# A fused Fourier-mixer block on one core: the order of all operations from a list scheduler that models the five queues

## The chip, the core and the metric

The kernel runs on one core of a Trainium2 chip. The core has five engines with a queue each: TensorE (PE, with its weight loads as PEld), VectorE (DVE), ScalarE (ACT), GpSimd (POOL) and SyncE (SP, which here only issues transfers). Each works through its own queue in the order in which the program was built, and semaphores make it wait for the others. The metric is the device time of one execution in microseconds (us), lower is better. Before the change the median of 3 runs is 2781.52 us (2774.99 to 2794.49).

## What is computed

The input is `x`, 8 x 128 x 128 x 96 in float32. After a layer norm over the channels, a filter in frequency space and a residual, a second layer norm feeds a small two-layer network on values rounded to 8-bit floats, and a second residual ends the block. Cut to what matters:

```
x_pre = soa(einsum('bhwc,mc->bhwm', x, w1))            # 96 -> 192 channels; soa(x) = scale * relu(x)^2 + bias
xf    = rfft2(x_pre)                                   # over h and w, 128 x 65 frequencies
filt  = [Rh @ cw_s @ Rw for s in range(3)]             # three small complex filters, resized to 128 x 65
gctx  = x.mean((h, w)); sctx = relu(bn(x @ sp_w.T)).mean((h, w))
r     = softmax(mlp([gctx, sctx]), over the 3 filters) # per batch and channel
comb  = einsum('shwm,bsm->bhwm', filt, r)
out   = einsum('bhwm,cm->bhwc', irfft2(xf * comb), w2)
```

and for the network `y = qlinear(relu(qlinear(z, W1, b1)), W2, b2)` with 96 -> 384 -> 96 channels, where both operands of a product are rounded to fp8 (5 exponent bits) and sums to fp16.

## The kernel before

The Fourier transforms are matrix products with constant matrices. The work of each of the 8 batches is cut into three streams that pass their results through DRAM.

- **Stream a** (`before`, from L618), 32 steps u of 4 columns. Layer norm statistics are made on DVE (`measure`, L635) and POOL; the factor goes to DRAM and comes back spread over partitions (`store_r`, `load_r`, L643 to L649), `scale` (DVE, L651) applies it to the transposed input `zT`. `project` (PE, L663, writes `px`), `rectify` and `square` (ACT) and `context` (POOL) make `x_pre`; `transform` (PE, `py`, L693) is the transform over h; `put` (ACT) and `store_y` write Y to DRAM. At the end of a batch nine small steps `rate_*` (L744 to L805) make the softmax weights.
- **Stream s** (`spectrum`, from L825), 33 groups g of frequencies. `load_y` (SP, four transfers a group) and `load_t` fetch Y and the filters `tb`; `weigh` (POOL, L855) applies the batch's weights; `along_w` (PE, `pz`, L863) is the transform over w; `filters_of` (PE, `pf`, L865) resizes the filters; `copy_sr` (ACT), `make` and `times` (DVE, L900 and L903), `turn_back` and `real_basis` (POOL) multiply by the filter. For each of 16 pairs p of groups, `mix_low` and `mix` (PE, `pv`, L958) project 192 channels to 96, `mixed` (ACT) copies, `invert` (PE, `pg`, L978) transforms back, `inverted` (ACT) copies, `store_v` writes V.
- **Stream c** (`after`, from L1066), 32 steps u in 8 blocks of 4. `load_v` fetches x and V, `last` (PE, `pk`) is the last transform back, `residual` and `measure` (DVE) follow, then the layer norm's `variance`, `root`, `inverse`, `rest`; `quantise` (ACT, for the last batch half of it on DVE), `turn` (PE, transposes), `turned` (DVE), `first` (PE, `ph`), `accumulated` (ACT), `biased` (DVE), `hidden` (ACT), `second` (PE, `po`), `put` (ACT), `bias` (DVE), `add_up` (POOL), `store`.

Stream s of a batch needs all of its stream a, and stream c all of its stream s. So in the middle of the run stream a of one batch, stream s of the one before and stream c of the one before that are interleaved. `filters_of`, `mix_low` and `mix` use 64 columns of PE's array with 52 or 64 rows, so that four products share it (the 64-wide tiling); all other products use the whole array or take it as one tile.

**What sets the order.** Each operation is handed to `at` (L388) with a wished time, the operations that it needs (`after`), how many of the 6 PSUM banks it takes and which operations set them free (`until`). Wished times are written out: a start and a length for each stream of each batch (`STREAMS`), and an offset in steps for each kind of operation (`O`, with own tables for four of the streams, `OWN`). `in_order` (L323) takes from a heap the operation with the lowest time whose needs have been taken, and skips one for which no bank is free:

```
place[follower.key] = max(place[follower.key], place[op.key] + lag)   # lag 0.15, or 2.28 for a transfer
heappush(ready, (place[follower.key], follower.seq, follower))
```

It has no notion of how long an operation lasts or of what its engine is doing. The list that comes out is built in that order, and L1243 ties each engine's instructions to it. Waits on data, and on buffers that are used again, are added as the program is built.

## Time and profile before

| | us |
|---|---|
| median of 3 runs | 2781.52 (2774.99 to 2794.49) |
| the profiled execution | 2788.19 |
| its span | 2786.4 |
| mean granted PE clock in it | 0.958 of full |
| DMA queue of SP, of ACT: share of 16 engines' span | 60.7%, 14.4% |
| PE waiting on its longest named cause (`px` for the scaled `zT`) | 38.5 |
| SP waiting for stores of `t` (POOL), for Y's buffers (PE `pz`), for the norm's factor to come back | 266.0, 200.3, 106.5 |

The profile lists matmuls under the tile that they write: `px`, `py`, `pz`, `pf`, `pv`, `pg`, `pk`, `ph`, `po` as named above (`pz<-ident` is the transpose `turn`). A float32 product has two records. An engine's busy time is the union of its records; PE's records overlap, [...]so the length of one is more than what it takes from PE. "Idle before" is an engine's idle time ahead of an operation, and the name after the arrow is what ended it.

### The profile page before, as it was taken

To read this page: it belongs to the slowest core of one execution; us is meant where nothing else is said; L and a number is where in the kernel's file an instruction comes from. 1 tells how busy PE (TensorE), PEld (TensorE's weight loads), DVE (VectorE), ACT (ScalarE), POOL (GpSimd) and SP (SyncE) were. 2 spreads that over 40 slices of the span, in tenths; PEclk is the share of its full clock that TensorE was granted. 3 is DMA by queue.
4 is the path that set the end of the run, shared out by engine and by line. 5 is a ranking of instruction groups with operands and counts; after the bars stand their busy time and mean duration, and the time that the engine had idled before them with its cause. 6 is when DMAs were issued, how large, how long until landed. Compare 5 with 4: busy or idle time off the path is not lost.

```text
span 2786.4 us, 80592 instructions
## 1 busy us (share of the span) xinstructions
PE 2545.2 (91%) x30762; PEld 1887.8 (68%) x30762; DVE 2035.8 (73%) x5110; ACT 2210.3 (79%) x4452; POOL 2063.5 (74%) x2983
## 2 busy tenths in 40 slices
PE   4879999999999999999999999999999998898665
PEld 2557777677677767776677777777767776676433
DVE  3346666577877778786787779677887768888686
ACT  2665555588888888888998878789988987788887
POOL 2228886778788877887788869888788886998432
PEclk9899999999999999999999999999999998999886
DMA  7888888978689867887788858888788775665431
GB/s 203 258 253 241 245 247 240 268 224 250 204 256 260 232 202 219 255 252 225 234 253 267 238 167 236 261 257 254 236 244 264 216 212 168 182 192 159 159 125 46
DMA packets 752818, 620.43 MB, mean 223 GB/s; under 512 B 578367, under 2 KB 654023, under 8 KB 752411
## 3 DMA queue, kind: packets, MB, share of 16 engines
q1 hardware_dynamic: 697138, 464.28, 60.7%
q10 hardware_dynamic: 55296, 151.02, 14.4%
q8 instruction: 244, 4.00, 0.6%
q14 instruction: 140, 1.14, 0.1%
HBM read 406.99 MB, written 208.16 MB: 221 GB/s over the span
## 4 chain that ended last, share of the span: by engine, by line
PE 60%; ACT 10%; POOL 9%; DMA 9%; DVE 6%; issue 5%; SPq 1%; ACTq 0%; POOLq 0%; DVEq 0%
PE px L666 12%; PE pz L863 9%; PE py L695 9%; PE pv L958 8%; PE pf L874 5%; PE pg L980 4%; PE ph L1128 3%; PE pk L1085 3%; PE po L1150 3%; ACT y L1135 3%; POOL t L1168 2%; ACT h L1143 2%; DMA tb<-T 2%; ACT z L1109 2%; POOL rr L911 2%
## 5 line engine op out<-in xcount | busy, mean ns | idle before, releaser
L911 POOL TENSOR_TENSOR rr<-t,t 128x390 f32<-128x390 f32 x512 | 536.7, 1058 | 58.5 <-DVE t L904 57.5
L666 PE MATMUL px<-W1S,zT 97*128 97x240 f32 x2048 | 521.7, 380 | 44.1 <-DVE zT L653 38.5
L1109 ACT ACTIVATE z<-t,ln_m,ln_r 128x96 fp8e5<-128x96 f32 x960 | 465.1, 495 | 43.5 <-DMA zT<-in_xT 11.7
L1135 ACT CAST y<-ph 128x512 f16<-128x512 f32 x768 | 458.0, 606 | 37.4 <-PE ph L1128 19.4
L666 PEld LDWEIGHTS px<-W1S,zT 97*128 97x128 f32 x2048 | 377.0, 194 | 141.9 <-issue 37.7
L863 PEld LDWEIGHTS pz<-F,yt 128*128 128x128 f32 x3120 | 417.0, 194 | 82.3 <-DVE t L1091 9.0
L863 PE MATMUL pz<-F,yt 128*128 128x130 f32 x3120 | 443.0, 282 | 13.2 <-DVE t L1091 6.0
L695 PE MATMUL py<-X,F 128*128 128x384 f32 x1024 | 432.1, 509 | 8.6 <-ACT yst L702 3.9
L677 ACT ACTIVATE rl<-px 128x480 f32<-128x480 f32 x512 | 296.3, 582 | 179.1 <-PE px L666 147.8
L1143 ACT ACTIVATE h<-y 128x1536 fp8e5<-128x1536 f16 x256 | 387.5, 1514 | 5.5 <-DVE y L1139 3.8
L857 POOL TENSOR_TENSOR tb<-tb,r 128x384 f32<-128x384 f32 (+1 forms) x264 | 296.7, 1124 | 124.3 <-DMA tb<-T 66.7
L1168 POOL TENSOR_TENSOR t<-t,o 128x1536 f32<-128x1536 f32 x64 | 206.1, 3221 | 188.9 <-DVE o L1165 185.3
L904 DVE TENSOR_TENSOR t<-dm,pf 128x390 f32<-128x390 f32 x512 | 283.2, 553 | 68.8 <-PE pf L874 39.0
L1139 DVE TENSOR_TENSOR y<-y,b1q 128x1536 f16<-128x1536 f16 x256 | 288.2, 1126 | 56.1 <-ACT y L1135 55.5
L958 PEld LDWEIGHTS pv<-w2C,xf 64*64 64x64 f32 x12288 | 274.2, 136 | 77.0 <-issue 32.9
L958 PE MATMUL pv<-w2C,xf 64*64 64x96 f32 x12288 | 315.8, 251 | 7.3 <-ACT yst L702 2.8
L1128 PE MATMUL ph<-zT,W1q 96*128 96x512 fp8e5 x768 | 297.4, 401 | 22.2 <-DVE zT L1124 8.8
L702 ACT COPY yst<-py 128x384 f32<-128x384 f32 x512 | 248.0, 490 | 70.1 <-PE py L695 57.6
L904 DVE TENSOR_TENSOR t<-dp,pf 128x390 f32<-128x390 f32 x512 | 280.6, 548 | 0.0
L928 POOL TENSOR_TENSOR xf<-rr 128x378 f32<-128x378 f32 x256 | 263.0, 1027 | 19.7
L926 POOL TENSOR_TENSOR xf<-rr 128x390 f32<-128x390 f32 x256 | 260.0, 1016 | 0.0
L874 PEld LDWEIGHTS pf<-RW,tb 52*64 52x64 f32 x6240 | 173.3, 133 | 109.9 <-issue 55.8
(117 smaller groups left out, 4460.4 us busy)
## 6 DMA issues: line engine op xcount, KB each, us to landing
yt<-Yd SPq DMA_DIRECT2D x1040, 96.0 KB
Yd<-yst ACTq DMA_DIRECT2D x256, 384.0 KB
xb<-in_xw SPq DMA_DIRECT2D x64, 768.0 KB
zT<-in_xT SPq DMA_DIRECT2D x128, 384.0 KB
rB<-Rd SPq DMA_DIRECT2D x128, 384.0 KB
tb<-T SPq DMA_DIRECT2D x256, 192.0 KB
Vd<-gst ACTq DMA_DIRECT2D x128, 384.0 KB
t<-in_x SPq DMA_DIRECT2D x64, 768.0 KB
```

The lines of the kernel that those rows point to most:

```text
L666: nc.tensor.matmul(px[:, i * (MED + SCTX) : (i + 1) * (MED + SCTX)], lhsT=zTs[(b * NU // 2 + u // 2) % NZT][:, QW * (u % 2) + i0 + i, :], ...
L695: nc.tensor.matmul(py, lhsT=F1, rhs=kept["X", u][:, i0 : i0 + 2, :].rearrange("h w m -> h (w m)"), start=True, stop=True)
L857: nc.gpsimd.tensor_tensor(kept["tb", g][p, :], kept["tb", g][p, :], rates[b][p, :], ALU.mult)
L863: nc.tensor.matmul(pz[:, q * 2 * L : (q + 1) * 2 * L], lhsT=y, rhs=F2[:, cs, :], start=True, stop=True)
L874: nc.tensor.matmul(pf[64 * k : 64 * k + 64, s, q * 2 * L : (q + 1) * 2 * L], lhsT=tb[p, m0 : m0 + 64], rhs=RW[p, :], start=True, stop=True,)
L904: nc.vector.tensor_tensor(work(name, g), kept[d, g], pair(g, sign, c), ALU.mult)
L911: nc.gpsimd.tensor_tensor(kept["rr", g][:, :, 2 * i : 2 * i + 2, :], kept[ta, g], kept[tb, g][:, :, ::-1, :], op)
L958: nc.tensor.matmul(kept["pv", p, r][half, i * C : (i + 1) * C], lhsT=kept["xf", g][rows, cs, q, half], rhs=w2C[rows, q, :], start=(i == 0 ...
L1109: nc.scalar.activation(z, t, AF.Identity, bias=m, scale=r, saturate=False)
L1128: nc.tensor.matmul(kept["ph", u, n], lhsT=W1q[:, n * 128 : (n + 1) * 128], rhs=kept["zT", u], start=True, stop=True)
L1135: nc.scalar.copy(kept["y", u][:, n, :], kept.pop(("ph", u, n)))
L1143: nc.scalar.activation(kept["h8", u], kept["y", u], AF.Relu, saturate=False)
```

## The change

The tables `STREAMS`, `OWN` and `O` go. In their place stand a start and length for each stream of each batch, one offset for each kind of operation, and a table with engine and duration of each kind:

```diff
-STREAMS = {
-    "a": ((-2.3, 125.8), (125.5, 235.3), (361.7, 294.9), (654.8, 258.7), (914.4, 293.7), (1208.1, 250.0), (1549.9, 242.8), (1792.3, 246.3)),
...
+WINDOWS = {
+    "a": ((-936.8, 194.3), (238, 493.5), (298, 631.8), (287.8, 272.8), (151.8, 28.3), (1074.4, 615.4), (1423.4, 389), (1781, 473.3)),
...
+WAIT, PATIENCE, TURN = (0.09, 0, 0.4, 0.14, 1.26), (7.44, 4.02, 8.15, 0.416, 53.7), 38.96
...
+PE, ACT, DVE, POOL, SP = range(5)
+COST = {
+    "a_project": (PE, 0.975, 0),
+    "a_transform": (PE, 0.809, 0),
+    "a_rectify": (ACT, 0.57, 0),
...
+    "s_load_y": (SP, 3.2, 1.728),
...
+QUARTER = {"s_filters_of", "s_mix_low", "s_mix"}
```

`in_turn` adds, for each kind of operation, that a step needs the whole step before it. `in_order` becomes a list scheduler: it keeps the time at which each of the five queues, each bank and the transfers would be ready, and takes again and again, on the engine that could start first, the operation with the lowest score among those that could start within `WAIT` of the first; on PE a change of tiling (`QUARTER`) costs score:

```diff
+            for i in able[e]:
+                if e == PE:
+                    t = last[PE] - (MODES[2] if mode and quarter[i] else MODES[1] if mode != quarter[i] else MODES[0])
...
+                t = max(t, ready[i])
+                if ops[i].banks:
+                    if len(open_banks) < ops[i].banks:
+                        continue
+                    t = max(t, open_banks[ops[i].banks - 1])
+                found.append((t, i))
+            if found:
+                first = min(found)[0]
+                lowest = 1e30
+                for t, i in found:
+                    if t <= first + WAIT[e]:
+                        score = place[i] + PATIENCE[e] * (t - first)
+                        if e == PE and quarter[i] != mode:
+                            score += TURN
...
+        if moves[i] > 0:
+            ring = max(f + LAND[0], ring) + moves[i]
+            end[i] = ring + LAND[1]
```

Needs for buffers that are used again are written out where they were left to the build, for example:

```diff
-                at(t + o["a_load_x"] * P - 6, load_x, blk, after=after)
-                rstd(t + o["a_rstd"] * P, o["a_step"] * P, "a", blk, kept, 1e-6, one)
-                at(t + o["a_store_r"] * P, store_r, blk, after=[one("rest", blk)])
+                if blk == 0:
+                    after.append((("a", b - 2), "rate_v0"))
+                at(t - 0.006, load_x, blk, after=after)
+                rstd(t, 0.3 * P, "a", blk, kept, 1e-6, one, [one("store_r", blk - 2)])
+                at(t, store_r, blk, after=[one("rest", blk)] + [one("load_r", 2 * blk + i - 6) for i in range(2)])
...
-            at(t + o["a_store_y"] * P + 0.5, store_y, u, after=both("put", u))
+            at(t + 0.0005, store_y, u, after=both("put", u) + [(("s", b - 3), "load_y", g) for g in range(NG + 2)] * (u < 3))
```

What the operations do, their tiles, buffers and number stay as they were; the order on all five queues is new.

## The prediction, made before the changed kernel was run

> **What bounds the kernel now.** I read the shares of the page first, then the slices, then busy time by stage.

> ```profile
> PE 2545.2 (91%) x30762; PEld 1887.8 (68%) x30762; DVE 2035.8 (73%) x5110; ACT 2210.3 (79%) x4452; POOL 2063.5 (74%) x2983
> PE   4879999999999999999999999999999998898665
> PEclk9899999999999999999999999999999998999886
> 0.00:200.00 200.00, 142.36 (x513) 97.28 (x513) 77.28 (x286) 100.84 (x193) 47.24 (x142) 0.93 0.77 237
> 200.00:2300.00 2100.00, 2023.51 (x25408) 1527.90 (x25407) 1577.38 (x3964) 1710.72 (x3486) 1704.30 (x2413) 0.98 0.82 239
> 2300.00:2600.00 300.00, 260.97 (x4066) 195.13 (x4066) 249.37 (x545) 247.63 (x504) 255.62 (x323) 0.95 0.58 167
> 2600.00:2786.40 186.40, 118.36 (x780) 67.48 (x779) 131.75 (x316) 151.09 (x272) 56.33 (x106) 0.74 0.35 115
> ```

> The stage lines give PE, PEld, DVE, ACT and POOL busy, then the granted clock, the DMA share and GB/s. PE is the bound for 2100 us (2023.5 busy). Around that lie a head (DMA share 0.77, PE 142 of 200), a stage with the last spectrum (2300 to 2600, all engines near 85%) and a tail where ACT leads (151 of 186).

> A busy PE is not a PE at its peak, so I price its operations from start to start, in the timeline.

> ```profile
> 1501.59 0.81 PE L1085 MATMUL pk<-vin,GK 128*128 128x384 f32 x2
> 1502.24 0.97 PE L666 MATMUL px<-W1S,zT 97*128 97x240 f32 x4
> 1503.14 0.90 PE L874 MATMUL pf<-RW,tb 52*64 52x130 f32 x24
> 1503.97 0.39 PE L1128 MATMUL ph<-zT,W1q 96*128 96x512 fp8e5 x1
> 1504.19 0.39 PE L1114 MATMUL pz<-ident,z 128*96 128x128 fp8e5 x4
> 1504.42 0.86 PE L695 MATMUL py<-X,F 128*128 128x384 f32 x2
> ```

> The first column is the start. `pk` takes 1502.24 - 1501.59 = 0.65, `ph` 0.22, `pz` (turn) 0.23; `px` ahead of `pf` takes 0.90. Medians over the trace at full clock, followed by work of the same tiling: project 0.812, transform 0.647, along_w 0.67, filters_of 0.716, half a mix 1.041, invert and last 0.648, turn 0.225, first 0.22, second 0.512. Ahead of a change between whole-array work and the 64-wide work of `pf` and `pv`, the same operations take 0.094 (into `pf`, `pv`) or 0.110 (out of them) longer.

> Times the counts: 512 x 0.812 = 416, 512 x 0.647 = 331, 520 x 0.67 = 348, 264 x 0.716 = 189, 256 x 1.041 = 266, 512 x 0.648 = 332, 256 x 0.225 = 58, 768 x 0.22 = 169, 256 x 0.512 = 131, others 22: **2262 us** of PE work. The other 524 us of the span are loss:

> - tiling changes: 932 in the built order, 466 pairs x 0.204 = 95;
> - 0 to 200: 120 of work, 80 lost;
> - 200 to 2300: 1847 of work, 253 lost: changes 80, clock 0.02 x 2100 = 42, so 131 of waits (76.5 idle as shown[...]);
> - 2300 to 2600: 223 of work, 77 lost: changes 12, clock 15, waits 50;
> - 2600 to 2786: 72 of work, 114 lost.

> Who ends the middle's waits, by PE's own waits between 200 and 2300:

> ```profile
> PE po L1150 <- ACT h L1143: 9.0, 11, 1.9
> PE pl L776 <- DVE hrep L771: 7.1, 3, 2.9
> PE ph L1128 <- ACT y L1135: 6.9, 2, 4.0
> PE px L666 <- DVE zT L653: 5.9, 3, 5.2
> PE pz L1114 <- ACT z L1109: 5.3, 9, 1.3
> ```

> No single wait matters: it is many short ones, a few us each in total, mostly an ACT result that came late because ACT was at something else.

> [...]

> **The change part by part.** Arithmetic, tiles and counts are the same in both builds (17813 matmuls, 1970 SP and 384 ACT transfers). All five queues are reordered.

> (1) *Fewer tiling changes.* The built order has 560 instead of 932: 91 pairs of mix halves now follow filters_of in one block, where none but 3 did. 372 x 0.102 = **38 us** off PE, 364 of them in the middle, where PE is the bound. Nothing hides PE there, so this counts in full.

> (2) *Queues that respect one another.* Before, an operation stood by its wished time alone, whatever its engine was doing. Now each engine takes what can start first. I counted in both built orders how much PE work lies between dependent operations. Before, almost none is too short: of 131 us of waits, only some 2 are forced by PE's own order, so the rest comes from other queues. In the new order the forced part grows: filters_of follows the last one by under 2.4 us (the four `times` on DVE, 4 x 0.55, must fit) 21 times, short by 16 us in sum; banks are taken again under 0.75 us 34 times, 8 us; project to transform 5, first to second 5: 35 us. To that I add 15 for late loads (below) and 30 for what differs from the scheduler's costs: 80 instead of 131, **-51**. Both ends: the 35 alone (-96), and no relief at all with the forced part on top (+35). I take -51 because the producers' distances are otherwise longer (scale to project 42 us of PE work on the mean, was 4.6; storing Y to loading it for the next stage 94, was 6; store_r to load_r 47, was 2.3, and SP waited 106 us for that round trip).

> (3) *Clock.* The 42 us follow the gaps: in proportion 42 x 80/131 = 26, and I take 30, **-12**; ends 0 and -27.

> (4) *The last spectrum with its neighbour, 2300 to 2600.* Work left on each engine is alike in both orders (with 270 us of PE work to go: ACT 449 and 453, DVE 369 and 372, POOL 281 and 284), so only the 50 us of waits can shrink: **-10**, ends 0 and -30.

> (5) *Head.* Transfers bound it, and the new SP order brings more forward: at 100 us of PE work, transfers worth 147 us of the 16 engines stand ahead instead of 127. At a share of 0.8 that is 25 us, but 0.87 to 0.89 was reached between 200 and 400 us, and what came early is not due later. **0**, ends -10 and +20.

> (6) *Tail.* After the last spectrum's last copy, ACT has 155 us of batch 7 and 33 of batch 6 left, before 155 and 31; batch 7 can't load V sooner in either. **0**, ends -8 and +8.

> (7) *New needs* (store_r after load_r, root after quantise, store_y after load_y three batches earlier) name waits that shared buffers impose anyway: **0**. Event waits on PE go from 1066 to 1140; even 0.05 us each would be 4.

> (8) *Loads nearer to their use*, the risk. Load_y stands 12.9 us of PE work ahead of its along_w in the median (before 22.1), 6.4 in the lowest tenth, 3.7 at least; 78 of 240 under 8, before none. Four issues of 0.62 and, by matching bytes issued to bytes moved in the packets, 2.9 us (4.8 in one of ten) to landing make 5.4 to 7.3 us: most are in time. The 15 us in (2) are for this.

> Sum: 38 + 51 + 12 + 10 = 111. Against the profiled span 2786.4 - 111 = 2675. The profiled execution took 2788.2, the median is 2781.5; so 2781.5 - 111 = **2670 us**.

> **Rivals.** *More goes:* all waits of the middle but the forced 35 (96), the clock's 27, 30 in the last spectrum and 38: 191, so 2590. For it speaks that no wait is large; against it that DMA was at 0.82 of its engines in the middle and comes nearer to 0.87.

> *The waits come back in another queue:* PE keeps only the 38, less some of the forced 35: about 2770, within 1%. ACT's own records (busy 1711 of 2100 us in the middle) leave room, which speaks against it.

> *Slower: PE stands at loads.* 78 loads of Y and 38 of the filters have under 8 us of lead. PE is in order, so each late one stops everything. With them 1.5 us late on the mean, 116 x 1.5 = 174 eats the gain: 2781.5 - 111 + 174 = 2845. It decides from 0.96 us late (111 / 116), and is over 1% slower from 1.2 us. For it: [...]SP issues in order. Against it: the 5.4 us above.

> *The order isn't what runs:* excluded, each engine's order is pinned in both builds.

> **How the numbers follow.** 1% of the median (2754 to 2809) is about what a measurement can tell from no change. Forecast (2610 to 2735): 0.53. Smaller gain down to 1%: 0.07. More goes: 0.20. Within 1%: 0.10. Slower: 0.10. So faster by over 1% 0.80, within 0.10, slower 0.10. The forecast's own range is 2610 to 2735; the 8-in-10 range reaches to 2580 (most of the larger gain) and 2780 (half of no change).

> **What would show it.** Right: in the middle stage PE idle under 50 us where it was 76.5, `px`, `py` ahead of `pf` and `pv` in fewer, longer blocks, a clock of 0.99, a tail of 180 to 195 us, `PE px <- DVE zT` (38.5 us in all) nearly gone. Wrong: idle before `pz` or `pf` with `DMA yt` or `tb` as releaser over 60 us (the slower rival); DVE `t` and ACT waiting longer with PE as idle as before (no change); a head that reaches full PE work 20 us later.

## The result, and the profile after

After takes **2820.3 us** (median of 4, 2815.09 to 2825.23) beside 2785.2 for before on the same chip: ratio 1.0127, 95% interval 1.0084 to 1.017. The forecast was 2670 with a range of 2580 to 2780. The result lies outside it, and on the slower side of before. The profiled execution has a span of 2813.3 us, 27 more than that of before, at a mean clock of 0.947 (0.958).

From the page of after, the shares and two rows of the slices:

```profile
PE 2525.7 (90%) x30762; PEld 1905.1 (68%) x30762; DVE 2092.1 (74%) x5110; ACT 2210.2 (79%) x4452; POOL 2066.3 (73%) x2983
PE   5778998989999899999999999899999998988675
PEclk9689999999999999999999999999999999999766
```

PE is busy 20 us less than before, over a longer span. Counted in the two traces, tiling changes fell from 936 to 566, so they did go. But the row starts with 5778998 (slices of 70 us) where before had 4879999, and the clock row has a 6 in its second slice. By stage, with the columns as in the prediction:

```profile
0.00:200.00 200.00, 136.43 (x415) 87.84 (x416) 83.72 (x351) 77.52 (x157) 55.59 (x180) 0.85 0.77 230
200.00:2300.00 2100.00, 1986.72 (x25144) 1529.19 (x25146) 1612.33 (x3900) 1704.19 (x3466) 1674.31 (x2359) 0.98 0.81 239
2300.00:2600.00 300.00, 266.84 (x4220) 203.87 (x4213) 248.58 (x528) 253.56 (x516) 259.48 (x317) 0.94 0.58 169
2600.00:2813.30 213.30, 135.70 (x998) 84.22 (x994) 147.44 (x332) 174.94 (x317) 76.88 (x129) 0.72 0.32 108
```

From 200 to 2300 us, the stage called the middle, PE stands idle 113.3 us, not under 50 (before 76.5). In the head the clock fell from 0.93 to 0.85 at the same DMA share. The tail looks longer only because the run reaches it later: from the last PE operation of the last spectrum to the end it is some 196 us, before 193. PE's own waits from 200 to 2300 are again many and short:

```profile
PE po L1258 <- ACT h L1251: 13.6, 9, 4.4
PE pf L983 <- DVE t L1013: 13.2, 10, 2.3
PE pz L972 <- DMA yt<-Yd: 9.9, 5, 3.4
```

The transfer of Y, the slower rival's place, is worth 9.9 us in this stretch, where that rival wanted 174. Over the whole run `px` waiting for `zT` has gone from 38.5 to 10.1 us, as forecast.

Busy time says little here, so I priced all traces in the prediction's way. PE's records of a window times their start-to-start prices are *work*. *Changes* (`chg`) are tiling changes x 0.102. *Half* is half of the time at clock 0.5; the first 50 us or so of a run have no clock record and are counted as if they were at 0.5, for neighbouring matmuls of `px` start 0.400 us apart there as they do in half-rate stretches, and 0.203 apart at full rate (medians in before and after, 14 pairs of them in the first 50 us). *Waits* are what is left of the window. The work of a whole run is 2262 us in every order, so more work in a window is progress. `150` and `300` are the times at which PE had done that much work, and MB is what the DMA had moved by the first of them. Each row is one profiled execution of one kernel (the experiments below), and executions of one kernel lie 10 us and more apart, so a difference of a few us in a column means nothing by itself.

```
                    0 to 400 us             400 to 2300 us           2300 to 2600   head
                 work chg half waits    work  chg half waits        work waits    150  MB    300
before            300   8   42   50     1667   75   34  124         223   50      240  56.7  400
after             260   4   64   72     1687   42   31  139         232   41      272  64.1  451
m1 mix together   306   8   38   48     1665   59   27  149         221   54      234  56.9  395
h1 before's head  267   4   59   69     1674   42   34  149         234   39      265  64.1  440
h2 after's head   274   7   57   62     1670   75   24  131         232   45      269  63.7  428
f1 stats early    265   7   64   64     1677   75   22  126         231   45      267  62.7  437
w1 weights early  269   5   54   73     1684   42   31  143         228   44      265  63.9  441
h3 first loads    270   5   54   71     1690   42   31  137         226   47      262  64.2  434
nudge             265   4   57   73     1644   41   48  167         214   59      270  64.2  442
u1 mix apart      272   7   49   72     1641   61   37  160         234   40      258  64.6  439
p2 other clock    280   5   61   55     1699   47   26  128         221   48      260  63.9  422
p3 other clock    284   5   54   57     1683   48   32  136         222   49      258  64.1  420
```

After is 40 us of work behind at 400 us, wins 20 back by 2300 us and 9 in the last spectrum. The 11 us of work that are still missing at 2600 us cost 27 us of time, because in the tail PE does little work per us (some 72 us of work in before's last 186 us).

### The profile page after: what moved, and what is told of

The parts are those of the page before. It is cut to its first block, busy times and chain, and to the rows that moved or that the text cites. A ratio compares the mean times of both kernels' runs of the same rounds, so it can differ in the third digit from the quotient of the medians.

```text
span 2813.3 us, 80718 instructions
## 1 busy us (share of the span) xinstructions
PE 2525.7 (90%) x30762; PEld 1905.1 (68%) x30762; DVE 2092.1 (74%) x5110; ACT 2210.2 (79%) x4452; POOL 2066.3 (73%) x2983
## 5 line engine op out<-in xcount | busy, mean ns | idle before, releaser
L772 PE MATMUL px<-W1S,zT 97*128 97x240 f32 x2048 | 491.2, 382 | 21.5 <-DVE zT L759 10.1
L1243 ACT CAST y<-ph 128x512 f16<-128x512 f32 x768 | 412.6, 607 | 34.8 <-PE ph L1236 27.7
L801 PE MATMUL py<-X,F 128*128 128x384 f32 x1024 | 402.3, 512 | 33.8 <-ACT rl L783 10.4
L972 PE MATMUL pz<-F,yt 128*128 128x130 f32 x3120 | 418.6, 284 | 14.3 <-DMA yt<-Yd 9.9
L1217 ACT ACTIVATE z<-t,ln_m,ln_r 128x96 fp8e5<-128x96 f32 x960 | 414.7, 482 | 13.6 <-POOL ln_m L717 9.5
L1247 DVE TENSOR_TENSOR y<-y,b1q 128x1536 f16<-128x1536 f16 x256 | 316.6, 1243 | 75.6 <-ACT y L1243 74.4
L1010 DVE TENSOR_TENSOR dm<-pz,sr 128x390 f32<-128x390 f32 x256 | 143.0, 559 | 194.2 <-ACT sr L1006 102.4
L797 POOL TENSOR_TENSOR sacc<-sacc,rl 128x192 f32<-128x192 f32 x248 | 173.1, 698 | 147.4 <-ACT rl L783 142.0
L801 PEld LDWEIGHTS py<-X,F 128*128 128x128 f32 x1024 | 185.2, 196 | 135.8 <-ACT rl L783 16.4
L983 PE MATMUL pf<-RW,tb 52*64 52x130 f32 x6240 | 240.0, 282 | 34.0 <-DVE t L1013 14.0
```

Source lines behind the costliest of these rows:

```text
L772: nc.tensor.matmul(px[:, i * (MED + SCTX) : (i + 1) * (MED + SCTX)], lhsT=zTs[(b * NU // 2 + u // 2) % NZT][:, QW * (u % 2) + i0 + i, :], ...
L801: nc.tensor.matmul(py, lhsT=F1, rhs=kept["X", u][:, i0 : i0 + 2, :].rearrange("h w m -> h (w m)"), start=True, stop=True)
L972: nc.tensor.matmul(pz[:, q * 2 * L : (q + 1) * 2 * L], lhsT=y, rhs=F2[:, cs, :], start=True, stop=True)
L1217: nc.scalar.activation(z, t, AF.Identity, bias=m, scale=r, saturate=False)
L1243: nc.scalar.copy(kept["y", u][:, n, :], kept.pop(("ph", u, n)))
L1247: nc.vector.tensor_tensor(y, y, b1q, ALU.add)
```

## Experiments

Ratios are to before on the same chip (medians 2779 to 2782), with 95% intervals; after's is 1.0127. "Written out" means that `in_order` returns a fixed list and nothing else of the kernel of after is altered; the diffs of these runs show the rule by which the list was made, not lines of the kernel. Where the order of before is taken, a few operations stand a little later, as the new needs ask.

**Tiling changes alone (m1).** The order of before written out, each `mix` directly behind its `mix_low`; changes 932 to 762.

```diff
-mix_low p, (other work), mix p
+mix_low p, mix p, (other work)
```

> The order of before written out, with each mix moved to stand directly behind its mix_low, and nothing else moved: changes of tiling fall from 932 to 762. If a change of tiling costs PE 0.102 us and PE is the bound, 170 x 0.102 = 17 us less than before (0.6%). If the gain of fewer changes is taken back by later results of the moved operations (the rival), no difference to before, or slower.

Measured 2779.1 us, 0.9993 (0.9974 to 1.0012): the second branch. The table shows where the 17 us went: from 400 to 2300 us changes fell by 16 and half clock by 7, and waits rose by 25. In the traces of before, m1 and after each engine runs the same instructions equally often, event waits apart, so the kernels differ in the order alone. What the new needs cost through the order is not tested: a written-out list does not consult them.

**Tiling changes the other way (u1).** The order of after written out, 138 operations of 64-wide work put one product later; changes 560 to 822.

```diff
-filters_of g, mix_low p, mix p, (product)
+filters_of g, mix_low p, (product), mix p
```

> The order of after in which the last operation of each block of 64-wide work, where a block has several, stands one whole-array product later: 138 operations are moved by some 0.7 us each, and tiling changes on TensorE go from 560 to 822. At the measured 0.102 us a change that is 27 us. If PE's own work is what paces the middle, after gets 25 to 30 us slower (2845 to 2850). If the other engines pace it as much, the time comes out of waits as it did in the order of before, where 170 changes fewer gave 2 us: within 10 us of after.

Measured 2858.4, 1.0288 (1.0245 to 1.0331): 1.6% or 45 us over after, more than the price of 27, though the two intervals together leave 28 to 62. From 400 to 2300 us changes rose by 19, half clock by 6 and waits by 21. So in the order of after added changes count. The moved operations also come later for those that wait for them, and the run does not separate this from the changes. In the order of before taking changes out gave nothing. PE's time alone paces neither.

**The head (h1, h2).** h1: before's order to the first `along_w` (632 operations), then the rest as after has it. h2: after's to that point (741), then the rest as before has it.

```diff
-return order
+return head + [op for op in other_order if op not in head]
```

> The order of before up to the first along_w of batch 0 (632 operations), then the rest in the order of after. If the loss lies in the head (after has done 40 us less PE work at 400 us), it ends some 35 us below after, near before (about 2785). If the head's early transfers for batches 1 and 2 are paid back later (the rival), it ends as after does, near 2820.

> The order of after up to the first transform over w of the first spectrum (741 operations), then all that is left in the order of before. If the first 200 us of the order of after are worth its loss by themselves (TensorE had done 98.5 us of work there against 120), this is about 20 us slower than before, 2805. If the loss is made between 200 and 400 us and in the fine order of the rest, it is within 10 us of before, 2780 to 2790.

h1 2817.4, 1.0155 (1.0121 to 1.0188): nothing gained. h2 2805.0, 1.0082 (1.0058 to 1.0106): 23 us lost, the first branch. Windows from the start to 150 and to 300 us of PE work, for before, after and h1, show what differs:

```profile
0.00:240.00 240.00, 177.00 (x958) 124.74 (x958) 102.71 (x353) 121.62 (x231) 76.04 (x184) 0.93 0.78 237
0.00:400.00 400.00, 336.62 (x3184) 250.54 (x3188) 200.84 (x605) 214.47 (x415) 214.95 (x376) 0.96 0.83 243
```

```profile
0.00:272.00 272.00, 197.14 (x856) 132.83 (x857) 122.31 (x463) 121.32 (x242) 90.01 (x242) 0.87 0.80 236
0.00:451.00 451.00, 363.12 (x3056) 263.16 (x3060) 227.98 (x731) 213.81 (x428) 226.42 (x431) 0.91 0.80 232
```

```profile
0.00:265.00 265.00, 186.17 (x854) 129.81 (x855) 121.73 (x463) 124.89 (x242) 90.59 (x242) 0.88 0.78 242
0.00:440.00 440.00, 348.93 (x3040) 258.18 (x3044) 225.99 (x730) 217.30 (x428) 226.94 (x431) 0.92 0.79 237
```

Time x rate (last column) gives the bytes: at 150 us of work before has moved 57 MB, after and h1 64, all at 0.236 to 0.242 MB/us. 7.4 MB are 31 us at that rate, and 272 - 240 = 32. h1 was ahead of before at 100 us of work (165 us against 177, 41.8 MB), then had to move 22 MB before the next 50 us of work were done. What is extra, by the loads issued in the traces: at 100 us of work 16 blocks of x for the statistics have been asked for where before had 12, at 150 us 21 and 13, at 300 us 27 and 19, at 0.79 MB each. The scheduler lets VectorE, idle in much of the head, take the statistics of later batches.

**Those statistics alone (f1).** The order of before written out, 113 operations (`load_x` to `store_r` of batches 1 and 2) put where after has them.

```diff
-load_x, measure, variance, root, inverse, rest, store_r at their place
+the same, where TensorE's work done is what it is in the order of after (to 160 us)
```

> The order of before in which the statistics of batches 1 and 2 (block of x, measure to store_r, 113 operations) stand where the order of after has them, up to 160 us of TensorE's work. In after 46.3 MB had moved when TensorE had done 100 us of work and 64.1 at 150, against 42.2 and 56.7 in before; seven blocks of x of 0.79 MB more at 100 us are most of it. If these early bytes are what holds TensorE up in the head, the same bytes show here, TensorE reaches 150 us of work some 20 to 30 us later than before's 240, and the run takes about 2800 to 2815. If the transfers only fill time that was free, it is within 8 us of before.

Measured 2818.3, 1.0128 (1.0093 to 1.0164): this alone makes the order of before as slow as after. The opposite run, after with these statistics put late, was not made. From the start to 150 and 300 us of PE work:

```profile
0.00:267.00 267.00, 188.86 (x958) 131.03 (x962) 119.21 (x450) 123.10 (x236) 90.89 (x234) 0.87 0.77 235
0.00:437.00 437.00, 352.12 (x3178) 258.63 (x3182) 210.19 (x646) 214.71 (x416) 226.41 (x395) 0.91 0.77 228
```

The time to 150 us of work is near that of after. At 400 us of work it has moved 125.0 MB, as before has (125.4): the early bytes are not due later, just as the prediction said. The time does not come back (546 us against 516). From 150 to 300 us of work PE is near its own pace in both, and the engines of the DMA are simply less busy (0.77 in f1, 0.89 in before):

```profile
240.00:400.00 160.00, 159.63 (x2226) 125.80 (x2230) 98.12 (x252) 92.85 (x184) 138.91 (x193) 1.00 0.89 253
267.00:437.00 170.00, 163.26 (x2232) 127.60 (x2224) 90.98 (x196) 91.61 (x180) 135.52 (x162) 0.97 0.77 219
```

The run shows that the early statistics cost the time, not by which way. The bytes are one. The queues are another: the statistics stand in four of them, and each was taken in order (in the trace of before ScalarE's 4435 computing instructions, VectorE's 4982, GpSimd's 2979 and SP's 1970 transfers start in the built order; so do PE's matmuls by their lines, but for 3 places among 3652 groups of one line). ScalarE stood 62 us at the square roots of the norm up to 150 us of work, in before 24, in after 46. These are its waits in f1 (to 267 us) and before (to 240 us), and the longest one with PE behind it (start, length, engine, operation, idle before):

```profile
ACT ln_r L594 <- DMA Rd<-ln_r: 34.8, 5, 13.4
ACT ln_r L594 <- POOL ln_v L589: 27.0, 3, 14.0
ACT ln_r L596 <- POOL ln_v L591: 24.0, 2, 14.9
174.90 0.22 ACT L594 ACTIVATE ln_r<-ln_v 128x16 f32<-128x16 f32 x1 [13.37 <-DMA Rd<-ln_r]
175.54 1.97 PE L663 MATMUL px<-W1S,zT 97*128 97x240 f32 x4 [10.36 <-ACT yst L699]
```

That square root is one of batch 1. It waited until the factor of two blocks before had been stored and its buffer was free. SP issued that store at 167.66 us, after it had stood in front of three loads of x. The copy `yst` that PE needed stood behind the square root on ScalarE. Up to 400 us SP waited 47.6 us in all for the buffers of such loads. Bytes, ScalarE's waits and SP's were not separated.

**Two stalls in the head (w1, h3).** The timeline of after shows VectorE and behind it PE:

```profile
116.07 0.36 DVE L651 CAST W1q<-w1f 96x384 fp8e5<-96x384 f32 x1 [10.30 <-DMA w1f<-in_W1T]
121.76 1.65 PE L801 MATMUL py<-X,F 128*128 128x384 f32 x2 [10.29 <-DVE tk L634]
```

`weights` issues its four loads and casts them at once, so VectorE waits for its own loads. w1 issues them 250 operations earlier; h3 also puts the zero padding and the first block of x behind the raw weights, where before has them.

```diff
+        def load_weights():
+            nc.sync.dma_start(out=w1f, in_=a["W1T"])
...
         def weights():
-            nc.sync.dma_start(out=w1f, in_=a["W1T"])
...
             nc.vector.tensor_copy(W1q, w1f, saturate=False)
```

> The order of after written out; only the four loads of the second network's weights are taken out of the operation weights and stand 250 operations earlier on SP, so that DVE no longer waits 10.3 us for them at 105.8 us with PE behind it. If PE's stalls in the head count in full, 8 to 13 us below after (about 2809). If the head is set by transfers (the rival), within 3 us of after.

> The order of after with two things put as before has them: the zero padding and the first block of x stand behind the loads of the raw weights, and the four loads of the network's weights stand 250 operations ahead of the casts that need them, as in the run with only that. TensorE's first wait was 17.1 us in after against 9.7 in before, its wait behind the casts 10.3. If the first 200 us of after lose their 20 us at these two places, this is 15 to 20 us faster than after, about 2800, and 98.5 us of work by 200 us become 112 or more. If the transfers as a whole set the pace there, the first place gives nothing beyond the 10 us that the weights' loads gave.

w1 2808.3, 1.0103 (1.0063 to 1.0143); h3 2806.0, 1.0099 (1.0061 to 1.0137). Either is some 7 us under after, between the two branches of w1, and the intervals overlap with it; the first loads add nothing beyond. Work by 400 us rose by 9 and 10. The same 64 MB had been moved at 150 us of work, but at 265 and 262 us instead of 272. So these stalls are a part of the head's loss, and the bytes alone do not set the time: over the ten orders with 62.7 to 64.6 MB it lies between 258 and 272 us, where the two with 57 MB need 234 and 240.

**Room for a late result.** A copy of one column more on VectorE behind each `times` (1024), or on ScalarE behind each `accumulated` (768), in both orders.

```diff
             nc.vector.tensor_tensor(work(name, g), kept[d, g], pair(g, sign, c), ALU.mult)
+            nc.vector.tensor_copy(scrap, soa_bias)
...
             nc.scalar.copy(kept["y", u][:, n, :], kept.pop(("ph", u, n)))
+            nc.scalar.copy(scrap, soa_bias)
```

> The order of before, with one more VectorE copy of one column behind each of the 1024 products with the filter (a copy of this size took 0.134 us in the trace of before, so up to 137 us more for an engine that was busy 2036 of 2786 us). Nothing waits for the copy itself; it only makes what VectorE does next come a little later. Theory A (the order of before has room between a result and its use, the order of after is laid out to the tenth of a microsecond on its own clock and has none): before loses little, 5 to 30 us. Theory B (both orders have the same room, and after is slower for its first 400 us and nothing else): before loses what after loses in the twin of this run.

> The order of after with the same 1024 copies of one column. Theory A (no room in the order of after): 50 to 90 us above after, so about 2870 to 2910, and at least twice what before loses. Theory B (the same room as before): the same loss as before within 10 us.

> The order of before with one more ScalarE copy of one column behind each of the 768 accumulated copies, some 0.2 us each, so about 150 us more for an engine that was busy 2210 of 2786 us. The same amount on VectorE cost 9 us. If ScalarE paces the middle beside TensorE (most of TensorE's named waits end with one of its results), this costs 40 us or more. If there is room on every engine but TensorE, it costs about 10 as on VectorE.

> The order of after with the same 768 ScalarE copies. If ScalarE paces the middle in this order too, 40 us or more above after. If the order of after leans on ScalarE harder than that of before does, clearly more than the twin loses, some 80 us. If TensorE alone paces it, about 10.

By tile, the copies on VectorE and ScalarE in the order of after (ns: least, median, most):

```profile
L1015 DVE COPY scrap<-soa_bias x1024: 134/147/151, 240.6 to 2611.1; 128x1 f32<-128x1 f32 x171
```

```profile
L1245 ACT COPY scrap<-soa_bias x768: 188/218/398, 549.4 to 2841.9; 128x1 f32<-128x1 f32 x192
```

Records overlap (VectorE's in before sum to 2369 us, over 2036 busy), so VectorE's busy time rose by only 55 us in before and 65 in after, ScalarE's by 61 and 63. VectorE: before 2790.9, 1.003 (1.0013 to 1.0047), 8 us lost; after 2823.2, 1.013 (1.0096 to 1.0163), 1 us over after, give or take 15. Theory A, that the order of after breaks where the order of before has room, fell. ScalarE: before 2801.7, 1.0071 (1.0048 to 1.0095), 20 us; after 2847.8, 1.0246 (1.0213 to 1.0279), 1.2% or 33 us over after. Both lost less than the 40 us and more than the 10 that the branches named. A third to a half of ScalarE's added time reaches the end, so ScalarE shares the pace; that after leans on it harder is not shown, as the intervals overlap.

**The scheduler's clock (nudge, p2, p3).** While it builds the order the scheduler keeps a clock of its own. It ends at 2648 us for after. Put through the same model, the order of before ends at 2944, though the chip runs it faster. nudge changes one constant:

```diff
-WAIT, PATIENCE, TURN = (0.09, 0, 0.4, 0.14, 1.26), (7.44, 4.02, 8.15, 0.416, 53.7), 38.96
+WAIT, PATIENCE, TURN = (0.0899, 0, 0.4, 0.14, 1.26), (7.44, 4.02, 8.15, 0.416, 53.7), 38.96
```

> after with WAIT for PE 0.0899 instead of 0.09: the scheduler's own plan then ends at 2751 us instead of 2648, by its own clock, with 554 changes of tiling. If the chip follows the plan, it is some 100 us slower than after (about 2920). If the plan's differences of that kind are not real (the rival: constants fitted to the plan), it ends within 30 us of after (2790 to 2850).

Measured 2887.1, 1.0394 (1.0349 to 1.0439): 74 us over after where the clock says 103 (2751 against 2648), between the two branches and nearer to the first. Put through the scheduler alone, other small changes of PE's `WAIT` and of the first number of `LAND` end at 2688 to 2751 on that clock, and none earlier than after: its constants sit at a low point of this clock.

p2 and p3 are written-out orders from the same scheduler with other constants, found by a corrected clock, whose three corrections were fitted to before, after, m1, h1 and nudge. For the third, the last section gives what the traces show.

```diff
-end of a result + REACH, moves, one PE rate
+end of a result + REACH + 0.1, 0.6 x moves, half rate for 3.41 us after such a window under half busy
```

> An order from the scheduler of after with other constants, chosen out of some thousand by a corrected clock: every result reaches another engine 0.1 us later than the scheduler's table says, transfers take 0.6 of what it says, and TensorE runs at half rate for a 3.41 us window after one in which it was busy under half. 618 tiling changes. By the scheduler's own clock this order is 130 us worse than that of after (2778 against 2648). By the corrected clock it is 124 us better (2670 against 2794, and 138 better than the order of before, 2808). If the wrong step is in what the clock leaves out, this runs about 2680 to 2730, ahead of both kernels. If the scheduler's clock ranks orders rightly and the chip adds its 166 us to any, it runs at about 2900 or more.

> A second order from the scheduler with other constants, found from another start than the first: results reach other engines 0.22 us later than the scheduler's table says, transfers take 0.85 of what it says and land 0.5 us later; 628 tiling changes. The corrected clock of the first such run puts it at 2679 (first run 2670, chip 2765), the scheduler's own clock at 2765 (that of after 2648). If the corrected clock ranks orders rightly and errs by some 90 us on orders that were chosen by it, this runs at 2765 to 2785, not slower than before. If the first run was luck, it is as slow as after or slower, 2815 or more.

p2 2764.5, **0.9944 (0.9929 to 0.996)**: ahead of both kernels, of before by 15 us, but not at the 2680 to 2730 that were expected. By the table it loses 20 us of work against before in the head and wins 32 from 400 to 2300 us, where changes fell by 28 and half clock by 8 while waits stayed (124 and 128): in this order the saved changes did count. p3 2788.9, 1.0042 (1.0026 to 1.0059): ahead of after, but behind before and 4 us above the range it was given, so its expectation was missed. The 2778 and 2765 that the two texts call the scheduler's own clock contain the half-rate windows; without them it gives 2742 and 2729. The figures of both clocks are calculated outside the chip. How a written-out list is put through the scheduler's clock moves its figure by up to some 70 us (another way gives 2999 for before and 2704 for p3). All in one view, profiled spans of the chip last:

```
                    before after   m1    h1    h2  nudge   u1    f1    p2    p3
scheduler's clock    2944  2648  2940  2725  2932  2751  2764  3029  2742  2729
corrected clock      2808  2794  2818  2842  2812  2945  2897  2883  2670  2679
chip                 2786  2813  2783  2815  2809  2897  2856  2816  2763  2787
```

On these ten orders, most of them made from others of the ten, the scheduler's clock says nothing of the chip's ranking (rank correlation -0.05). The corrected one has 0.82, and 0.90 (plain correlation) over the five that it was not fitted to. It still puts after ahead of before, which is the wrong way round, and which of its three corrections matters was not tried. And each clock is too early most of all on what it chose: the first by 165 us on after, the second by 93 and 108 on p2 and p3, where on the other eight it lies between 19 too early and 67 too late.

## Why the prediction was wrong, step by step

In spans the forecast was -111 and the result +27. Over the whole run changes gave -38, half clock took 31 (142 to 173) and waits 34 (287 to 321).

1. *Fewer tiling changes, -38*: the size is right (95 to 57 us), and u1 shows that added changes cost time in this order. "This counts in full" is not general: m1 got 2 of 17 in the order of before.
2. ***Queues that respect one another, -51*: the first step that failed.** From 400 to 2300 us waits went from 124 to 139. I took 131 us of waits (76.5 idle, the others a difference whose cause no view shows) as order conflicts that a scheduler dissolves, and judged the relief by how much PE work lies between dependent operations. Those distances did grow, and `px <- zT` did go. None of the twelve orders has under 124 us of waits there. ScalarE's added time shows that a second engine shares the pace, which speaks for short waits that take one another's place; that 124 us is a floor is not shown. What it consists of in single causes, and why after has 139, stays open.
3. *Clock, -12*: +31, of which 22 in the head and 12 after 2300 us. The step followed the waits with the right sense; it failed with (2) and (5).
4. *Last spectrum, -10*: right (work 223 to 232).
5. ***Head, 0, ends -10 and +20*: the second step that failed.** The count came true in size: by 100 us of PE work the DMA engines had been busy for 0.77 x 203 = 156 us in after and 0.78 x 177 = 138 in before, 18 more where the step said 20. That early bytes are not due later is right in bytes (f1). Wrong was that early statistics cost nothing: f1 loses 38 us by them alone (h2, with the whole head of after, 23), and later PE is near its own pace and cannot pay the time back. 300 us of work are reached at 451 us, not 400. The step weighed bytes alone; that the early statistics also make SP and ScalarE stand, with PE behind them, was not in it, and how the loss divides between the two is open. The warning sign that the prediction named, a head 20 us later, is what came.
6. *Tail, 0*: right (193 and 196 us).
7. *New needs, 0*: not tested by themselves. PE's event waits did go from 1066 to 1140 as counted; the median record of one takes 0.051 us in both traces.
8. *Loads nearer to their use*: `pz <- DMA yt` is 9.9 us, within the 15 allowed; that the slower rival ends on the right side is luck, for its mechanism did not come.

So of the 138 us between forecast and result, 44 were lost in the first 400 us (waits and half clock 22 each), 75 from 400 to 2300 (waits 15 instead of -51, clock -3 instead of -12), and 19 after that. The change does what it says, but on a clock that does not rank orders as the chip does; that it leaves out the half rate after gaps and weighs transfers and hand-overs wrongly is what the better ranking of the corrected clock suggests.

## What to carry to other kernels

Where a list scheduler gives an idle engine whatever can start, it pulls loads and statistics of later work forward. Count what is asked for ahead of each piece of the bottleneck engine's work, and look at what the other in-order queues then stand at: here such early work cost 38 us, and the stage after it, with PE near its own pace, did not return the time. Before an order that a model chose is trusted, put the old order through the same model: if the model does not rank the two as the chip does, its gain can be its own error. And PE time saved or added where PE is busy 96% of the stage changed the time by between nothing (m1) and its price or more (u1), depending on the order around it; try the part alone.
